# A Winograd-like 3x3 convolution with attention: its VectorE operations chained with the softmax, and a 1x1 convolution moved into the middle of the 3x3

## The chip, the cores and the metric

One core of a Trainium2 chip runs the kernel. The metric is device time in microseconds (us) from one launch; lower is better. The five engines each execute their own queue of instructions in the order in which they stand: TensorE (PE, with its weight loads shown apart as PEld), VectorE (DVE), ScalarE (ACT), GpSimd (POOL) and SyncE (SP, which here issues nearly all DMAs).

## The reference

Input x is 8 images of 512 channels, 32x32, in float32. Two layers run one after the other, each with a residual:

```python
x = x + L0(_gn(x))       # _gn: group normalization, 32 groups of 16 channels
x = x + L1(_gn(x))       # L1: one 1x1 convolution, weights scaled and masked by softmax gates, channels permuted

def L0(x):
    t = cbs(x, cv1_w, cv1_bn, 0)             # 1x1, batch norm, silu: 512 -> 512
    ys = [t[:, :256], t[:, 256:]]
    for i in range(2):                       # two blocks
        yi = ys[-1]
        z = cbs(yi, m_cv1_w[i], m_cv1_bn[i], 1)                    # 3x3, 256 -> 256
        z = bot_attention(z, m_qkv_w[i], m_rw[i], m_rh[i])         # 4 heads of 64, 1024 positions
        z = silu(bn_eval(conv2d(z, m_cv2_w[i], 0), m_cv2_bn[i]))   # 1x1, 256 -> 256
        ys.append(yi + z)
    return cbs(concatenate(ys), cv2_w, cv2_bn, 0)                  # 1x1, 1024 -> 512
```

The attention adds a position term to k, takes logits over 1024x1024 positions, a softmax over the keys and the product with v.

## The kernel before

Work is cut into 16 slots, one for each (image, block). Images go in pairs: (0, block 0), (1, block 0), (0, block 1), (1, block 1), then images 2 and 3, and so on. I number slots from 0, so that a slot s with s mod 4 of 2 or 3 is a block 1 slot. A slot's foreground is its attention, as four `Unit`s (two pairs of heads, two halves of the 1024 queries). For each of eight key tiles a unit does:

- `logits` (L487-505): two matmuls `lg` into two PSUM banks, two ScalarE copies to the SBUF tile `st` (L500), two VectorE maxima `mx` that read the same banks (L505).
- After tile 7, `top` and `spread`: TensorE transposes `mt` of `mx`, a VectorE reduction (L514), TensorE transposes `mb` (L521).
- `soften` (L523-531): VectorE adds the negated maximum to `st` (L525), ScalarE takes the exponential (L526), GpSimd accumulates the denominators `sum` (L531).
- `values` (L537): two matmuls into `po`. At the end come `den`, a ScalarE copy `rb` (L551), and VectorE's reciprocal and product (L556, L558).

Between these steps a filler, `slot_filler(s)` (L871-904), hands out TensorE work of other kinds, by a budget of estimated microseconds (`SHARE`, 103 in a slot): the next slot's 3x3 convolution (`conv3`) and q, k, v projections (`project`), the 1x1 convolution `conv_m2` behind a finished attention, and background items from `bg` (`conv1`, 1x1 `cv` from x; `conv2`, `cv` from y; `last`, `l`). Every `yield` hands the turn back with the estimated time of what was emitted.

`conv_m2(i)` has four tiles: two matmuls into a bank `m2` each (traced as four instructions, "m<-q"), a silu on ScalarE (`m2s`, L130), a VectorE residual add (L406) and a store. In the slots before a block 1 slot the filler runs conv_m2(0), which makes that slot's input image; conv_m2(1) belongs to the previous slot's image when that one was in block 1 (s mod 4 of 3 or 0). After it, `finishing` adds that image's `conv2` and `last` to the background list.

The 3x3 convolution is done as six products over transformed rows:

- `transform` (L236-268) makes eight VectorE operations on the padded image `ybuf`, as a `Spread`: due times by the emission clock, with `upto(n)` forcing the first n. L256-L257 make `a` and `b`, L258-L259 planes 1 and 2, L261-L262 `a2` and `b2`, L263-L264 planes 3 and 4. For a block 0 image two slots ahead it is scheduled at the end of the filler, 8 us later and 1.3 us apart, after `load_y` has issued the load of `ybuf`.
- `conv3` (L270-350) runs products 1, 2, 3, 4, 0, 5 in this order, each 12 matmuls into one bank ("m<-plane", twice as many instructions in the trace) with four yields in all. After product 2, L316 and L317 combine it with product 1 on VectorE, L319 and L320 start planes u0 and u5 on GpSimd, and L321 and L322 finish them on VectorE. L328-L329 combine products 3 and 4, a second `Spread` (L330-339) of four VectorE operations prepares the sums, L343 and L347 add products 0 and 5, and two silus on ScalarE finish `z` (L349).

What sets the order on an engine: the program is emitted in the order of these generators, and a scheduler then orders each engine's instructions by priority and readiness as it estimates it. Instructions can be tied by an explicit dependency without a semaphore. Before the change, only `mx` (L505) and `st` (L525) are tied so: each is kept behind the one that was emitted before it, by `in_turn` (L469-475).

Buffers: `ps_f` has five PSUM banks, which `lg`, `mt`, products, `m2`, `cv`, `l`, `qk`, `v` and `den` take in the order of emission; `po` and `mb` have their own. A new tile waits until the last reader of the bank's previous tile is done. Weights have four SBUF buffers. The core has one `ybuf`, four planes and three temporaries `wt`.

Of the kernel before, what the change touches and what calls it, by code (L numbers as in the profile page):

```python
# [17 lines left out]
ALU = mybir.AluOpType  # L18
AX = mybir.AxisListType
PSUM = bass.MemoryType.PSUM  # L20
IN_ORDER = mybir.DependencyInfo(mybir.DependencyClass.NoSync, mybir.DependencyReason.DATA)
# [18 lines left out]
def conv_preact_kernel(ctx: ExitStack, tc: tile.TileContext, x, cv1, cv2, mcv1, qkv, mcv2, bn, rw, rh, conv, s_in, t_in, out):  # L40
    nc = tc.nc
    stt = nc.vector.scalar_tensor_tensor
# [22 lines left out]
    def pair(p, tag, name):  # L65
        return p.tile([P, 2, HALF], F32, tag=tag, name=name)

    def bank(name):
        return ps_f.tile([P, HALF], F32, tag="bank", name=name)
# [10 lines left out]
    def weights(name, shape, src):  # L80
        t = wp.tile([P, *shape], F32, tag="w", name=name)
        load(t, src)
        return t
# [45 lines left out]
    def bn_silu(dst, src, col):  # L129
        nc.scalar.activation(dst, src, AF.Silu, bias=bn_b[:, col : col + 1], scale=bn_s[:, col : col + 1])  # L130
# [40 lines left out]
    def accumulate(ps, terms):  # L171
# [5 lines left out]
                yield 1.72  # L177
        return Whole(1.72)

    class Spread:  # L180


# [5 lines left out]
        def upto(self, n):  # L188
            while self.done < n:
                self.done += 1  # L190
                self.ops[self.done - 1]()

    class Image:
        def __init__(self, n):
# [75 lines left out]
        def conv3(self, i):  # L270
            n = self.n
            name = f"{n}_{i}"
            self.inputs.upto(3)
            t, d = self.t, self.d

            def plane():
                plane_count[0] += 1
                return planes[plane_count[0] % 4]

            def inner(u):  # L280
                return u[:, :, 1 : F + 1]

            def product(r, u):
                w = weights(f"w_m1_{name}_{r}", (IT, IT, 3, P), w_m1[i][r])
                ps = bank(f"m1_{name}_{r}")
                terms = [(c, dx) for c in range(IT) for dx in range(3)]
                for co in range(IT):
                    for j, (c, dx) in enumerate(terms):
                        nc.tensor.matmul(  # L289
                            ps[:, ts(co, 256)].rearrange("p (t x) -> p t x", x=F),  # L290
                            w[:, co, c, dx],
                            u[:, 9 * c : 9 * c + 8, dx : dx + F],
                            start=(j == 0),
                            stop=(j == len(terms) - 1),
                        )
                        if j % 3 == 2 and (co, j) != (1, 5):
                            yield 1.33
                self.ps = ps

            z = self.z = qp.tile([P, IT, HW], F32, tag="z", bufs=1, name=f"z_{name}")  # L300
            y4 = z.rearrange("p c (t j x) -> p (c t) j x", j=4, x=F)
            y = [y4[:, :, j] for j in range(4)]

            def tx(ap):
                return ap.rearrange("p (g x) -> p g x", x=F)

            mm, ss, dd = (pair(wm, q, f"{q}_{name}") for q in ("mm", "ss", "dd"))
            yield from product(1, t[1])
            nc.scalar.copy(mm[:, 0], self.ps)
            yield 1.33  # L310
            self.inputs.upto(4)
            yield from product(2, t[2])
            self.inputs.upto(8)
            a, b = t["a2"], t["b2"]

            nc.vector.tensor_tensor(ss[:, 0], mm[:, 0], self.ps, ALU.add)  # L316
            nc.vector.tensor_tensor(dd[:, 0], mm[:, 0], self.ps, ALU.subtract)  # L317
            u0, u5 = plane(), plane()
            nc.gpsimd.tensor_tensor(inner(u0), d[0], d[2], ALU.subtract)  # L319
            nc.gpsimd.tensor_tensor(inner(u5), d[5], d[3], ALU.subtract)  # L320
            stt(inner(u0), inner(u0), 4.0, a, ALU.mult, ALU.add)  # L321
            stt(inner(u5), b, -4.0, inner(u5), ALU.mult, ALU.add)  # L322
            yield 1.33
            yield from product(3, t[3])
            nc.scalar.copy(mm[:, 1], self.ps)
            yield 1.33
            yield from product(4, t[4])
            nc.vector.tensor_tensor(ss[:, 1], mm[:, 1], self.ps, ALU.add)  # L328
            nc.vector.tensor_tensor(dd[:, 1], mm[:, 1], self.ps, ALU.subtract)  # L329
            sums = Spread(  # L330
                [
                    lambda: stt(y[2], tx(ss[:, 1]), 4.0, tx(ss[:, 0]), ALU.mult, ALU.add),
                    lambda: nc.vector.tensor_tensor(ss[:, 0], ss[:, 0], ss[:, 1], ALU.add),
                    lambda: stt(y[1], tx(dd[:, 1]), 2.0, tx(dd[:, 0]), ALU.mult, ALU.add),
                    lambda: stt(dd[:, 0], dd[:, 1], 8.0, dd[:, 0], ALU.mult, ALU.add),
                ],
                1.0,
                1.3,
            )
            yield 1.33  # L340
            yield from product(0, u0)
            sums.upto(2)
            nc.vector.tensor_tensor(y[0], tx(self.ps), tx(ss[:, 0]), ALU.add)  # L343
            yield 1.33
            yield from product(5, u5)
            sums.upto(4)
            nc.vector.tensor_tensor(y[3], tx(self.ps), tx(dd[:, 0]), ALU.add)  # L347
            for co in range(IT):
                bn_silu(z[:, co], z[:, co], BN_M1 + IT * i + co)  # L349
            yield 1.33  # L350
# [103 lines left out]
        def last(self, h, xn):  # L454
            n = self.n
            for cp in range(2):
# [8 lines left out]
                        yield us  # L465
                load(out[n, cp, :, :, ts(h, HALF)], res)
                yield us

    turn = []  # L469

    def in_turn(instruction):

        if turn:
            tc.add_manual_dep(instruction.ins, turn.pop().ins.name, IN_ORDER, reason="order of the softmax")
        turn.append(instruction)


    class Unit:
# [8 lines left out]
        def logits(self, t):  # L487

            if t == 0:
                self.begin()  # L490
            lg = [bank(f"lg_{self.name}_{t}_{h}") for h in range(2)]
            for h in range(2):
                r = slice(HD * h, HD * h + HD)
                nc.tensor.matmul(  # L494
                    lg[h], self.k[r, ts(t, P)], self.q[r, self.hp, ts(self.half, HALF)], start=True, stop=True
                )
            st = pair(stp, "st", f"st_{self.name}_{t}")
            self.st.append(st)
            for h in range(2):
                nc.scalar.copy(st[:, h], lg[h])  # L500
            if t == 1:
                self.mx = pair(one, "mx", f"mx_{self.name}")
            for h in range(2 if t else 0):
                so_far = self.st[0] if t == 1 else self.mx
                in_turn(nc.vector.tensor_tensor(self.mx[:, h], so_far[:, h], lg[h], ALU.max))  # L505
# [353 lines left out]
    def call(f, *a):  # L859
        f(*a)  # L860
        return
        yield

    def finishing(im):


        bg.add(Second(im, 0), Second(im, 1), held.pop(), Last(im, 0))
        held.append(Last(im, 1))
        bg.prepare()

    def slot_filler(s):  # L871

        prev = slots[s - 1] if s else (None, 0)
        nxt = slots[s + 1] if s + 1 < len(slots) else (None, 0)
        todo, needed = [], 0.0

        def add(us, g):
            nonlocal needed
            todo.append((us, g))
            needed += us  # L880

        im, i = nxt
        add(8.0, bg.take(8.0))
        if im and i == 1:
            add(7.0, im.conv_m2(0))
            add(0.0, call(im.transform, 1, 3.0, 1.0))
            add(9.0, bg.take(9.0))
        if im:
            add(32.0, im.conv3(i))
        if prev[1] == 1:  # L890
            add(7.0, prev[0].conv_m2(1))
            add(0.0, call(lambda: finishing(prev[0])))
        elif im:
            add(7.0, bg.take(7.0))
        if im:
            add(21.0, im.project(i))
        if s + 2 < len(slots) and slots[s + 2][1] == 0:
            add(0.0, call(slots[s + 2][0].load_y))
            add(0.0, call(slots[s + 2][0].transform, 0, 8.0, 1.3))
        rest = SHARE - needed if im else 70.0  # L900
        if rest > 0:
            todo.append((rest, bg.take(rest, wait=True)))
        total = sum(c for c, _ in todo)
        return needed, total, todo
# [73 lines left out]
    before = None  # L978
    for s in range(len(slots)):
        needed, total, todo = slot_filler(s)  # L980
        state = {"done": 0.0}

# [55 lines left out]
    im = images[NB - 1]  # L1038
# [55 lines left out]
```

## Time and profile before

| | |
|---|---|
| time, median of 3 runs | 3335.23 us (3323.23 to 3340.18) |
| the profiled execution | 3329.67 us, span 3328.0 us |
| mean granted TensorE clock | 0.985 |
| slots 4, 5, 6, 7 (they begin at 983.1, 1166.1, 1358.8, 1552.3 us; slot 8 at 1737.7) | 183, 193, 194, 185 us |
| one L525 `st`, L505 `mx`, L526 exp, L500 copy | 1212, 680, 1056, 595 ns |
| one `sum` of POOL (L531) | 1327 ns |
| TensorE instruction 128x512, full clock, half clock | 429 ns, 853 ns |
| DVE transform ops L256, 257, 258, 259, 261, 262, 263, 264 | 973, 1049, 1117, 714, 1387, 1046, 1256, 918 ns |

In rows of the profile, "out<-in" are the program's tile names; the numbers behind a bar are busy time in us, mean ns of one, and idle time just before the group with the instructions that ended it. In the timeline a line gives start, length, engine, line, tiles and count; in square brackets stands the idle time before it and what released it. L175 is the line of a helper (`accumulate`) and L130 that of `bn_silu`, so these are told apart by tile names.

### The profile page before, as it was taken

Reading aid. Unit: us, or ns where it says so; the run is one execution under the profiler, and the core shown is the slowest. Engines: PE = TensorE matmul, PEld = TensorE weight load, DVE = VectorE, ACT = ScalarE, POOL = GpSimd, SP = SyncE. Lnnn points to the kernel's source line nnn. Section 1 sums busy time; section 2 is a strip of 40 time slices with the busy share of each in tenths; the row PEclk is TensorE's granted clock in tenths of the full one; section 3 lists DMA queues with packets and bytes.
Section 4 is the critical chain, followed back from the end, with each engine's and each line's share of the span. In section 5 each row is a group of like instructions: output and inputs, shape, how many; then the busy total and the mean of one; then the engine's idle time right before and its main releaser. Section 6 shows DMA issues by size and latency. Waiting matters only on the chain.

```text
span 3328.0 us, 33287 instructions
## 1 busy us (share of the span) xinstructions
PE 3177.4 (95%) x11716; PEld 1541.6 (46%) x11716; DVE 2069.0 (62%) x2717; ACT 1763.7 (53%) x2371; POOL 1238.7 (37%) x971
## 2 busy tenths in 40 slices
PE   7999989999999999999999999999999999999998
PEld 3645344354445444354445445354545445353343
DVE  5536566666656566666656665776756665766642
ACT  3245765854555654644455554644455554645631
POOL 2114333445334443444334333434334343444420
PEclk9999999999999999999999999999999999999999
DMA  8752442421132241423232341423232341423366
GB/s 293 263 170 70 144 147 86 136 83 54 67 129 83 93 138 49 158 82 121 82 124 86 112 145 54 153 88 111 92 117 92 117 141 52 158 70 108 111 212 207
DMA packets 142006, 399.29 MB, mean 120 GB/s; under 512 B 13072, under 2 KB 14352, under 8 KB 141840
## 3 DMA queue, kind: packets, MB, share of 16 engines
q1 hardware_dynamic: 141120, 396.94, 34.8%
q8 instruction: 93, 1.52, 0.2%
q14 instruction: 73, 0.60, 0.1%
q10 hardware_dynamic: 720, 0.23, 0.0%
HBM read 317.42 MB, written 79.69 MB: 119 GB/s over the span
## 4 chain that ended last, share of the span: by engine, by line
PE 69%; DVE 10%; issue 6%; ACT 5%; DMA 3%; POOL 1%; SPq 0%; POOLq 0%; DVEq 0%; ACTq 0%
PE cv L175 14%; PE po L537 11%; PE m L289 11%; PE lg L494 11%; PE qk L175 6%; PE l L175 6%; PE v L381 3%; DVE st L525 2%; PE mt L513 2%; PE den L549 2%; PE m L175 2%; DVE mx L505 2%; PE mb L521 2%; ACT st L526 1%; DVE rb L556 1%
## 5 line engine op out<-in xcount | busy, mean ns | idle before, releaser
L531 POOL TENSOR_TENSOR sum<-sum,st 128x512 f32<-128x512 f32 x768 | 995.7, 1327 | 762.6 <-ACT st L526 762.6
L526 ACT ACTIVATE st<-st 128x1024 f32<-128x1024 f32 x512 | 536.2, 1056 | 516.9 <-DVE st L525 509.6
L505 DVE TENSOR_TENSOR mx<-mx,lg 128x512 f32<-128x512 f32 x768 | 479.2, 680 | 412.6 <-ACT st L500 412.2
L525 DVE TENSOR_TENSOR st<-st,mb 128x1024 f32<-128x1024 f32 x512 | 604.4, 1212 | 88.3 <-PE mb L521 88.3
L500 ACT COPY st<-lg 128x512 f32<-128x512 f32 x1024 | 527.3, 595 | 205.5 <-PE lg L494 163.8
L289 PE MATMUL m<-plane,w_m 128*128 128x256 f32 x2304 | 540.3, 388 | 24.3 <-DVE mx L505 18.6
L494 PE MATMUL lg<-q,k 64*128 64x512 f32 x2048 | 538.4, 620 | 10.6 <-ACT y L130 3.4
L537 PE MATMUL po<-st,v 128*64 128x512 f32 x2048 | 511.5, 611 | 7.5 <-ACT st L526 5.1
L289 PEld LDWEIGHTS m<-plane,w_m 128*128 128x128 f32 x2304 | 434.7, 193 | 148.9 <-issue 52.7
L531 POOL TENSOR_TENSOR sum<-st,st 128x512 f32<-128x512 f32 x128 | 160.3, 1274 | 878.9 <-ACT st L526 617.1
L175 PE MATMUL cv<-y,w_cv 128*128 128x512 f32 x1024 | 467.3, 600 | 3.0 <-ACT m2s L130 1.3
L494 PEld LDWEIGHTS lg<-q,k 64*128 64x128 f32 x2048 | 189.8, 186 | 349.3 <-issue 218.2
L175 PEld LDWEIGHTS cv<-y,w_cv 128*128 128x128 f32 x1024 | 185.1, 190 | 251.0 <-issue 235.5
L537 PEld LDWEIGHTS po<-st,v 128*64 128x64 f32 x2048 | 125.7, 137 | 328.3 <-issue 250.0
L556 DVE RECIPROCAL rb<-rb 128x256 f32<-128x256 f32 x128 | 216.0, 1725 | 71.9 <-ACT rb L551 71.9
L175 PE MATMUL l<-x,w_l 128*128 128x512 f32 x512 | 239.5, 614 | 17.0 <-DVE mx L505 12.3
L175 PE MATMUL cv<-x,w_cv 128*128 128x512 f32 x512 | 237.1, 610 | 17.3 <-DVE mx L505 9.0
L175 PE MATMUL qk<-z,w_qkv 128*128 128x512 f32 x512 | 236.7, 604 | 10.5 <-DVE mx L505 10.5
L514 DVE TENSOR_REDUCE nm<-mt 128x4 f32<-128x512 f32 x128 | 83.2, 685 | 189.2 <-PE mt L513 189.2
L130 ACT ACT_TABLE_LOAD x123 | 157.8, 1283 | 19.0 <-PE cv L175 8.1
L175 PEld LDWEIGHTS l<-x,w_l 128*128 128x128 f32 x512 | 95.0, 194 | 141.2 <-issue 105.5
L175 PEld LDWEIGHTS cv<-x,w_cv 128*128 128x128 f32 x512 | 94.6, 193 | 140.8 <-issue 107.2
(144 smaller groups left out, 2372.6 us busy)
## 6 DMA issues: line engine op xcount, KB each, us to landing
w_m<-w_m SPq DMA_DIRECT2D x96, 768.0 KB, 4.3
w_cv<-in_cv SPq DMA_DIRECT2D x90, 512.0 KB, 3.5
y<-y SPq DMA_DIRECT2D x64, 512.0 KB, 4.9
x<-in_x SPq DMA_DIRECT2D x56, 512.0 KB, 5.1
y<-y SPq DMA_DIRECT2D x64, 256.0 KB, 3.8
k<-r SPq DMA_DIRECT2D x32, 512.0 KB, 3.6
res<-y SPq DMA_DIRECT2D x32, 512.0 KB, 4.1
xr<-in_x SPq DMA_DIRECT2D x32, 512.0 KB, 4.1
```

Source lines behind the costliest of these rows:

```text
L130: nc.scalar.activation(dst, src, AF.Silu, bias=bn_b[:, col : col + 1], scale=bn_s[:, col : col + 1])
L175: nc.tensor.matmul(ps, w, moving, start=(n == 0), stop=(n == len(terms) - 1))
L289: nc.tensor.matmul(ps[:, ts(co, 256)].rearrange("p (t x) -> p t x", x=F), w[:, co, c, dx], u[:, 9 * c : 9 * c + 8, dx : dx + F], start=(j ...
L381: nc.tensor.matmul(ps[:, ts(j, P)], z[:, c, ts(4 * j4 + j, P)], w[:, c, 512 + P * hp : 512 + P * hp + P], start=(c == 0), stop=(c == IT - 1),)
L494: nc.tensor.matmul(lg[h], self.k[r, ts(t, P)], self.q[r, self.hp, ts(self.half, HALF)], start=True, stop=True)
L500: nc.scalar.copy(st[:, h], lg[h])
L505: in_turn(nc.vector.tensor_tensor(self.mx[:, h], so_far[:, h], lg[h], ALU.max))
L525: in_turn(nc.vector.tensor_tensor(st, st, flat(self.mb), ALU.add))
L526: nc.scalar.activation(st, st, AF.Exp)
L531: nc.gpsimd.tensor_tensor(self.acc[:, h], so_far[:, h], self.st[t][:, h], ALU.add)
L537: nc.tensor.matmul(self.po[HD * h : HD * h + HD], self.v[:, t, ts(h, HD)], self.st[t][:, h], start=(t == 0), stop=(t == KT - 1),)
L556: nc.vector.reciprocal(self.rb[:, r], self.rb[:, r])
```

## The change

Two things are done. First, `in_turn` moves up, and the operations of every `Spread` (the eight transform operations and the four sums) as well as L321 and L322 pass through it: on VectorE these now keep the order of emission among themselves and with `mx` and `st`. L316, L317, L328, L329, L343, L347, L406 and the background's VectorE operations remain free.

Second, in the six slots that have both a previous block 1 image and a next slot (3, 4, 7, 8, 11, 12), the filler runs the first 16 yields of `conv3`, which are products 1, 2, 3 and 4, then conv_m2(1) with `finishing`, then products 0 and 5. Before, conv_m2(1) followed all six. In these slots a `bg.take(7.0)` is now put behind the products, and the rest that the slot's background takes shrinks by the same amount, since `needed` grows by 7.

```diff
+    turn = []
+
+    def in_turn(instruction):
+
+        if turn:
+            tc.add_manual_dep(instruction.ins, turn.pop().ins.name, IN_ORDER, reason="order of VectorE")
+        turn.append(instruction)
+
     class Spread:
...
             while self.done < n:
                 self.done += 1
-                self.ops[self.done - 1]()
+                in_turn(self.ops[self.done - 1]())
...
-            stt(inner(u0), inner(u0), 4.0, a, ALU.mult, ALU.add)
-            stt(inner(u5), b, -4.0, inner(u5), ALU.mult, ALU.add)
+            in_turn(stt(inner(u0), inner(u0), 4.0, a, ALU.mult, ALU.add))
+            in_turn(stt(inner(u5), b, -4.0, inner(u5), ALU.mult, ALU.add))
...
-    turn = []
-
-    def in_turn(instruction):
-
-        if turn:
-            tc.add_manual_dep(instruction.ins, turn.pop().ins.name, IN_ORDER, reason="order of the softmax")
-        turn.append(instruction)
-
...
-        if im:
-            add(32.0, im.conv3(i))
+        products = im.conv3(i) if im else iter(())
         if prev[1] == 1:
+            if im:
+                add(21.3, (us for _, us in zip(range(16), products)))
             add(7.0, prev[0].conv_m2(1))
             add(0.0, call(lambda: finishing(prev[0])))
-        elif im:
+        if im:
+            add(10.7 if prev[1] == 1 else 32.0, products)
             add(7.0, bg.take(7.0))
```

## The prediction

> **What bounds the kernel now.** I read the page's busy shares first, then its costliest groups, then the list of waits, and last the timeline around TensorE's longest gaps.
>
> ```profile
> span 3328.0 us, 33287 instructions
> PE 3177.4 (95%) x11716; PEld 1541.6 (46%) x11716; DVE 2069.0 (62%) x2717; ACT 1763.7 (53%) x2371; POOL 1238.7 (37%) x971
> PE 69%; DVE 10%; issue 6%; ACT 5%; DMA 3%; POOL 1%; SPq 0%; POOLq 0%; DVEq 0%; ACTq 0%
> L289 PE MATMUL m<-plane,w_m 128*128 128x256 f32 x2304 | 540.3, 388 | 24.3 <-DVE mx L505 18.6 <-DMA w_m<-w_m 3.4 <-issue 1.7
> L175 PE MATMUL m<-q,w_m 128*128 128x512 f32 x256 | 128.6, 649 | 18.2 <-ACT m2s L130 17.1 <-DVE mx L505 1.1
> ```
>
> TensorE is busy 95%; the change adds and removes no matmul, so it can work on the 150.6 us (3328.0 - 3177.4) in which PE is idle, and on matmul time run at a low clock. The last two rows say where idle time sits: the 3x3 products (L289) lose most before `mx` (L505, VectorE), the 1x1 `conv_m2` (L175, m<-q) before its own silu on ScalarE. The list of waits names who holds them:
>
> ```profile
> PE m L175 <- ACT m2s L130: 17.1, 6, 3.7
> DVE a L256 <- DMA ybuf<-y: 27.2, 8, 8.5
> DVE plane L321 <- POOL plane L319: 31.7, 12, 4.4
> ```
>
> The second row is VectorE waiting for an image load at the head of its queue, where `mx` is stuck behind it. The timeline shows each kind once, first slot 7's conv_m2(1), then slot 6's product 3:
>
> ```profile
> 1612.83 1.98 PE L175 MATMUL m<-q,w_m 128*128 128x512 f32 x4 [0.36 <-DVE mx L505]
> ...
> 1619.23 2.37 ACT L130 ACTIVATE z<-z,bn_b,bn_s 128x1024 f32<-128x1024 f32 x2
> 1621.51 0.76 ACT L130 ACTIVATE m2s<-m,bn_b,bn_s 128x512 f32<-128x512 f32 x1
> ...
> 1622.32 5.84 PE L175 MATMUL m<-q,w_m 128*128 128x512 f32 x7 [3.71 <-ACT m2s L130]
> ```
>
> ```profile
> 1436.87 0.74 DVE L256 SCALAR_TENSOR_TENSOR a<-ybuf 128x544 f32<-128x544 f32 x1 [3.66 <-DMA ybuf<-y]
> 1437.53 1.78 DVE L257 SCALAR_TENSOR_TENSOR b<-ybuf 128x544 f32<-128x544 f32 x1
> 1439.23 2.46 DVE L505 TENSOR_TENSOR mx<-mx,lg 128x512 f32<-128x512 f32 x4
> ...
> 1439.96 6.39 PE L289 MATMUL m<-plane,w_m 128*128 128x256 f32 x21 [4.21 <-DVE mx L505]
> ```
>
> In the first, conv_m2's second tile wants a PSUM bank whose silu stands behind the table load and the two `z` silus that end the 3x3. In the second, L256 of the next image's transform waits 3.66 us for its load, all four `mx` wait behind it, and with them the bank that product 3 needs. After the first gap seven L175 matmuls take 5.84 us (0.83 each), where four took 1.98 (0.5) before it: the clock had halved.
>
> **The Trainium skill.** "TensorE: Matmul & The Clock Gate", What's actually happening: the array falls to half clock after an idle window of about 3.4 us and returns after a busy one. The trace agrees on the halving (matmul spacing 429 ns against 853 ns, in stretches of 3.41 or 6.83 us) but gaps of 2.0 us (1056.4, 1811.0) were followed by one too, so I charge it for gaps of 2 us and more. "SBUF — State Buffer", SBUF: two separate sides: VectorE with two SBUF inputs and GpSimd exclude each other. The trace agrees: L257 takes 0.7 us alone and 1.79 us beside POOL's `sum`. "PSUM — Partial Sum Buffer", Terms: two engines on one bank at once are an error. So copies and `mx` of a bank must take turns; the trace has `mx` waiting 423.1 us, 173 times, for ACT's copies. A bank is thus free only when `mx` has read it: late VectorE work stalls TensorE.
>
> **The change part by part.** I compared the order of instructions on each engine in the two built programs with the gaps of the trace. SP's and POOL's orders stay nearly the same: only w_m2 and the two `res` loads come earlier, w_qkv later and the finished stores earlier, all loads of 3.5 to 5 us with a product (5.2 us) or more of lead. I cost them nothing; without that lead, one load is 4 us. "After" below stands for that order.
>
> A, conv_m2(1) between products 4 and 5 in slots 3, 4, 7, 8, 11, 12. (Product 0 runs after it too.) Removed: the waits on m2s, and later ones on `mx` held by L406's wait for m2s. The PE timeline gives 3.72, 3.72, 3.72 (867.4, 1622.3, 2376.8), 1.98 three times (1056.4, 1811.0, 2562.9) and 2.38, 3.50, 1.84 (1072.6, 1828.3, 2576.8): 24.8 us. Half-clock beside them: busy time inside the low stretches, halved, is 2.9 + 1.7 + 2.6 + 1.7 + 1.7 = 10.6. Added: after, the first tile follows the `mb` transposes while ACT is idle; the second takes the bank that lg_0_0 had, free after ACT's rb (0.58), table load (1.28), two exps (1.06 each) and a copy (0.60). Set against the PE work between, it comes about 1.3 us late: 6 x 1.3 = 7.8. Bounds: 0 (ACT starts earlier) to 3.7 (the old wait again), 0 to 22. Gain 24.8 + 10.6 - 7.8 = 27.6.
>
> B, the transform of the next image after the products instead of among them (slots 2, 6, 10): chained, L256 cannot stand ahead of these `mx`. Gone: 2.66 + 4.21 + 4.21 (708.5, 1440.0, 2194.5) = 11.1, and three half-clock stretches of 3.4 us, halved: 5.1. Gain 16.2. It is late next in E.
>
> C, slots 1, 5, 9: `mt` waits 4.6 us for `mx` behind L261, L262, L263 (1217.5, 1972.4, 2719.4). After, L263 (1.67 us there) stands behind the last `mx`: 3 x 1.67 = 5.0, and one or two of the three half-clock halves of 1.7: take 2.6. Gain 7.6 (0 to 10).
>
> D, slots 2, 6, 10: l waits 3.5 us behind L261, L258, L259 and L262 (1396.3, 2151.1, 2898.1). After, only L256 to L258 stand ahead, but the other five and the residual's L433 and L139 then precede the next two `mx`, and product 1 waits about 3.7 us for one of their banks. Its start was 1406.7 and becomes 1403.8 plus that wait's half clock of 1.7: net gain 1.2 each, 3.6 (-5 to 8).
>
> E, where the moved transforms land: the last of the four units. In slots 2, 6, 10 that unit's VectorE is idle only some 7.3 us of 1526 to 1550, and eight ops of 8.46 us (means of L256 to L264) come in. I find the second and third `l1` tiles waiting 2.2 and 2.5 us for banks, plus 0.8 of low clock: 5.5 x 3 = 16.5. In slots 3, 7, 11 with longer 1x1 tiles, 0.8 x 3 = 2.4. Loss 18.9; bounds: 0 (the room suffices) and twice that.
>
> F, the chain itself. L321 and L322 now stand in emission order, L322 ahead of `st` 6 and 7. In slot 7 POOL's L320 ended at 1578.43 and `st` 6 began at 1576.36; it would begin at 1580.1, and `mx` 6 and 7 move from 1583.1 to 1584.2. The bank is wanted at 1585.8: hidden, with about 1 us to spare. For spots like it that I missed I charge one VectorE op of 0.68 us for each of 15 convolutions: 10 us (0 to 20).
>
> Sum: 27.6 + 16.2 + 7.6 + 3.6 - 18.9 - 10 = 26 us less. The profiled execution took 3329.67 us, 1.7 outside its span; 3329.7 - 26 = 3304. The median shown is 3335.23, 5.6 above that execution: **3309**.
>
> **The rivals.**
> 1. Given back: A and B are gained, but E costs double (37.8) and A's new bank wait is like the old (3.3 each, 20). For: VectorE is at 62% over the whole, but nearly full in the last units. Against: some slack remains there. Sum of gains: 35.4 (A before its own new wait) + 16.2 - 20 + 11.2 (C, D) - 37.8 - 10 = -5, so 5 us slower, which is no change: 3340.
> 2. Slower, one mechanism: L322 at the head of VectorE's queue waits for POOL's L320, and `st` 6 and 7 wait behind it, then exp, `mx`, and the bank for product 4. The wait list above has L321 waiting 31.7 us for POOL already, 12 times, up to 4.4. If L320 sits behind one more pair of `sum` (2 x 1.33 = 2.7 us), 1.0 is hidden and 1.7 shows, with 1.7 of half clock: 3.4 for each of 15, 51. Behind two pairs 4.3 + 1.7, 90. Between them 70 against the 36 before F: 3335 + 34 = 3369. It decides from about 36 / 15 = 2.4 us per convolution, L320 some 2 us later than now. Against: POOL's order stays, and it is idle 63%.
> 3. The conv_m2 move does nothing since ACT's queue holds m2s in its new place too, while B to F hold: -26 + 27.6 = +2, 3337. It is counted with the first.
>
> **How the numbers follow.** Forecast 0.52; given back, with the third, 0.25; slower 0.23. The unknown costs, each at its bad end, give 12 + 11 + 0 - 5 - 38 - 20 = 40 us slower; at the good end 35 + 16 + 10 + 8 = 69 faster. They won't all fall together: I take 60 faster to 23 slower than 3335, 3275 to 3358, leaving out most of the slower case. Half a per cent, 16.7 us, is about what can be told from no change here. Faster by more: most of the forecast and a little of the second: 0.54; within: 0.23; slower: 0.23.
>
> **What would show it.** A: in L175's m<-q row the 17.1 us on m2s falls under 8, and no 3.7 us gap stands in slots 3, 7, 11. B: L256's wait for ybuf (27.2) no longer has PE gaps after it. C: `mt`'s 13.8 us falls to 9 or less. E: new `l` gaps behind `mx` late in slots 2, 6, 10. F: L322 behind L320 waits longer, but PE gaps before product 4 stay absent. I am wrong if PE idle grows beyond 150.6, above all with `st` L525 late in products 2 to 4 of every slot.

## The result and the profile after

The changed kernel takes 3281.7 us (median of 5 runs, 3278.47 to 3286.18) against 3335.23; the ratio is 0.9845 (95% interval 0.9826 to 0.9865). Its profiled execution has a span of 3276.7 us, 51.3 less. I number lines as in the kernel after where its rows are shown: before's L256-L264 are L264-L272, L289 is L297, L316-L317 are L324-L325, L321-L322 are L329-L330, L332-L335 are L340-L343, L343 is L351 and L406 is L414.

The page's first lines, and the rows of the list of groups that answer to those of before:

```profile
span 3276.7 us, 33257 instructions
PE 3159.1 (96%) x11716; PEld 1538.0 (47%) x11716; DVE 2045.9 (62%) x2717; ACT 1756.6 (54%) x2369; POOL 1219.1 (37%) x971
```

```profile
L297 PE MATMUL m<-plane,w_m 128*128 128x256 f32 x2304 | 534.0, 386 | 18.0 <-DVE z L351 8.3 <-DVE mx L505 6.2 <-DMA w_m<-w_m 2.8
L175 PE MATMUL m<-q,w_m 128*128 128x512 f32 x256 | 121.4, 614 | 4.0 <-ACT st L500 4.0
L513 PE MATMUL mt<-ident,mx 128*128 128x128 f32 x512 | 73.3, 288 | 10.7 <-DVE mx L505 10.7
```

The same matmuls are executed. TensorE's idle time fell from 150.6 to 117.6 us (3276.7 - 3159.1), 33.0; its busy time fell by 18.3, and the granted clock tells why: halving the busy time inside each half-clock stretch gives 47.4 us lost before and 30.1 after. The 3x3 now loses 6.2 us on `mx` instead of 18.6, and conv_m2 nothing on its silu instead of 17.1. New are 8.3 us in which the 3x3 waits for L351, VectorE's addition of product 0. In the list of waits the load at the head of VectorE's queue is rare now, and GpSimd hardly holds VectorE:

```profile
DVE a L264 <- DMA ybuf<-y: 8.4, 1, 8.4
DVE plane L329 <- POOL plane L327: 3.6, 1, 3.6
DVE plane L330 <- POOL plane L328: 0.6, 1, 0.6
```

The timeline of slot 7's conv_m2(1), where the gap of 3.71 us had been:

```profile
1576.18 1.88 PE L175 MATMUL m<-q,w_m 128*128 128x512 f32 x4
...
1578.10 0.78 ACT L130 ACTIVATE m2s<-m,bn_b,bn_s 128x512 f32<-128x512 f32 x1 [8.78 <-PE m L175]
...
1579.14 0.58 ACT L551 COPY rb<-den 128x512 f32<-128x512 f32 x1 [0.27 <-PE den L549]
1579.75 1.28 ACT L526 ACT_TABLE_LOAD   x1
...
1580.92 1.99 PE L175 MATMUL m<-q,w_m 128*128 128x512 f32 x4
1581.04 2.00 ACT L526 ACTIVATE st<-st 128x1024 f32<-128x1024 f32 x2
1582.95 2.02 ACT L500 COPY st<-lg 128x512 f32<-128x512 f32 x4
...
1583.57 3.70 PE L175 MATMUL m<-q,w_m 128*128 128x512 f32 x8 [0.67 <-ACT st L500]
```

ScalarE sat idle for 8.78 us before the first `m2s`, so it runs at once. After it come rb, a table load, two exps and the copies, and the third of the four tiles waits for a copy: 0.67 us in place of 3.71, and too short for the clock to drop.

Summed by slot (the start of a slot is its first `mt`), the gain lies so:

```
slots                  predicted (A to E, without F)      measured
3, 4, 7, 8, 11, 12     A 27.6 - E 2.4            = 25.2       25.9
2, 6, 10, 14           B 16.2 + D 3.6 - E 16.5   =  3.3       15.7
5, 9, 13               C                            7.6       10.8
0, 1, 15, before 0     none                                   -1.1
```

A slot's length is not waiting alone, since TensorE work moves between slots too: busy time without the half-clock loss is 1.7 us less in the first row and 2.6 less in the third, and 4.0 more in the second.

### The profile page after: what moved, and what is told of

Read it like the earlier page. It is cut to its first block, busy times and chain, and to the rows that moved or that the text cites. A ratio compares the mean times of both kernels' runs of the same rounds, so it can differ in the third digit from the quotient of the medians.

```text
span 3276.7 us, 33257 instructions
## 1 busy us (share of the span) xinstructions
PE 3159.1 (96%) x11716; PEld 1538.0 (47%) x11716; DVE 2045.9 (62%) x2717; ACT 1756.6 (54%) x2369; POOL 1219.1 (37%) x971
## 3 DMA queue, kind: packets, MB, share of 16 engines
q1 hardware_dynamic: 141120, 396.94, 36.1%
## 4 chain that ended last, share of the span: by engine, by line
PE 69%; DVE 11%; issue 5%; ACT 4%; DMA 4%; POOL 1%; POOLq 0%; SPq 0%; ACTq 0%; DVEq 0%
PE cv L175 14%; PE m L297 12%; PE po L537 11%; PE lg L494 10%; PE qk L175 6%; PE l L175 5%; PE v L389 3%; DVE st L525 3%; PE mt L513 2%; PE m L175 2%; DVE rb L556 2%; DVE mx L505 2%; PE den L549 2%; PE mb L521 2%; DMA x<-in_x 1%
## 5 line engine op out<-in xcount | busy, mean ns | idle before, releaser
L531 POOL TENSOR_TENSOR sum<-sum,st 128x512 f32<-128x512 f32 x768 | 973.9, 1299 | 771.5 <-ACT st L526 771.5
L297 PE MATMUL m<-plane,w_m 128*128 128x256 f32 x2304 | 534.0, 386 | 18.0 <-DVE z L351 8.3
L297 PEld LDWEIGHTS m<-plane,w_m 128*128 128x128 f32 x2304 | 431.4, 191 | 142.7 <-issue 40.8
```

What stands on the lines that cost most here:

```text
L297: nc.tensor.matmul(ps[:, ts(co, 256)].rearrange("p (t x) -> p t x", x=F), w[:, co, c, dx], u[:, 9 * c : 9 * c + 8, dx : dx + F], start=(j ...
L531: nc.gpsimd.tensor_tensor(self.acc[:, h], so_far[:, h], self.st[t][:, h], ALU.add)
```

## The experiments

Each was timed against the kernel before on the same chip; ratios have 95% intervals. The kernel before has medians from 3333.01 to 3336.06 us on the chips used, so a difference of two or three us between versions from different chips says nothing.

**The two edits apart.** First the chain, with the filler as before:

```diff
-        products = im.conv3(i) if im else iter(())
+        if im:
+            add(32.0, im.conv3(i))
         if prev[1] == 1:
-            if im:
-                add(21.3, (us for _, us in zip(range(16), products)))
             add(7.0, prev[0].conv_m2(1))
             add(0.0, call(lambda: finishing(prev[0])))
-        if im:
-            add(10.7 if prev[1] == 1 else 32.0, products)
+        elif im:
             add(7.0, bg.take(7.0))
```

> The chained VectorE order alone; conv_m2(1) stays behind all six products, without the extra background take. Theory 1 (the two edits work in different slots and add): the gain of slots 5, 6, 9, 10, 13, 14 and 2 stays, about 26 us, and that of slots 3, 4, 7, 8, 11, 12, also about 26, goes: near 3309 us, ratio 0.992, with TensorE gaps of about 3.7 us before conv_m2's second tile in slots 3, 7, 11. Theory 2 (the order carries all, the move is idle without need): near 3283, 0.985. Theory 3 (the move carries all): near 3335, 1.00.

Measured: 3298.57 us, ratio 0.9897 (0.9883 to 0.9912). Then the filler's edit alone, with only `mx` and `st` chained.

> The move of conv_m2(1) with the extra background take alone; only mx and st are chained, as before. Theory 1 (the edits add): near 3309, 0.992, with mt still waiting about 4.6 us in slots 5, 9, 13 and l about 3.5 us in slots 6, 10, 14. Theory 2 (the order carries all): near 3335. Theory 3 (the move carries all): near 3283.

Measured: 3305.04 us, 0.9916 (0.9901 to 0.9931). So neither edit carries all. By slots, slots 2, 5, 6, 9, 10, 13 and 14 gain 28.1 us with the chain alone and lose 3.1 with the move alone; slots 3, 4, 7, 8, 11, 12 gain 29.3 with the move alone and 8.9 with the chain alone. The gains overlap: 35.8 + 29.3 = 65.1 against 52.7 with both (3334.37 - 3281.7). The timeline of the chain-only kernel, slot 7, shows where:

```profile
1604.58 2.37 ACT L130 ACTIVATE z<-z,bn_b,bn_s 128x1024 f32<-128x1024 f32 x2
1606.86 0.76 ACT L130 ACTIVATE m2s<-m,bn_b,bn_s 128x512 f32<-128x512 f32 x1
...
1607.67 4.56 PE L175 MATMUL m<-q,w_m 128*128 128x512 f32 x10 [2.31 <-ACT m2s L130]
```

The same wait on m2s behind the `z` silus, 2.31 us here and 3.71 before: the chain shortens by 1.4 a wait that the move takes away whole. My expectation of 3.7 there was wrong, and with it that the edits merely add.

**Is it the place or the extra take?** The chain, the extra 7 us of background in the six slots, and conv_m2(1) after all six products:

```diff
-        products = im.conv3(i) if im else iter(())
+        if im:
+            add(32.0, im.conv3(i))
         if prev[1] == 1:
-            if im:
-                add(21.3, (us for _, us in zip(range(16), products)))
             add(7.0, prev[0].conv_m2(1))
             add(0.0, call(lambda: finishing(prev[0])))
         if im:
-            add(10.7 if prev[1] == 1 else 32.0, products)
             add(7.0, bg.take(7.0))
```

> The changed kernel, but conv_m2(1) stays behind all six products; the extra background take of 7 us stays between it and the projections. If the place of conv_m2 gives the gain in slots 3, 4, 7, 8, 11, 12: near 3309, with the 3.7 us gaps before its second tile back. If the extra take gives it, by putting other matmuls between the last product and what waits for z: near 3285, and qk's waits stay away.

Measured: 3304.97 us, 0.9917 (0.9900 to 0.9933): the take without the move gains nothing over the chain alone (3298.57). The complement keeps the move and leaves the take out:

```diff
             add(10.7 if prev[1] == 1 else 32.0, products)
-            add(7.0, bg.take(7.0))
+            if prev[1] != 1:
+                add(7.0, bg.take(7.0))
```

> The changed kernel without the 7 us of background that the change puts between product 5 and the projections in slots 3, 4, 7, 8, 11, 12. If that take is idle for the time: 3282, within 6. If it covers the wait for z's silus (qk after product 5): 3292 or more, with qk waits back. If it costs, as 3304.97 against 3298.57 of the two runs with conv_m2 at the end hints: near 3276.

Measured: 3268.35 us, 0.9806 (0.979 to 0.9822), 13.4 below the changed kernel's median. The take is a loss inside the change. Part of it is seen in slot 8. The changed kernel's timeline there:

```profile
1783.12 3.16 DVE L414 TENSOR_TENSOR res<-res,m2s 128x512 f32<-128x512 f32 x2 [1.56 <-DMA res<-y]
...
1786.20 1.21 DVE L525 TENSOR_TENSOR st<-st,mb 128x1024 f32<-128x1024 f32 x1
1787.34 0.68 DVE L351 TENSOR_TENSOR z<-m,ss 128x512 f32<-128x512 f32 x1
...
1788.07 4.15 PE L297 MATMUL m<-plane,w_m 128*128 128x256 f32 x18 [2.12 <-DVE z L351]
```

conv_m2's residual add waits for its load, `st` waits behind it, L351 behind that, and product 5 needs the bank that L351 reads. Without the take the adds take 1.29 us together, beside no GpSimd sum, and L351 comes in time:

```profile
1777.88 1.29 DVE L414 TENSOR_TENSOR res<-res,m2s 128x512 f32<-128x512 f32 x2 [1.59 <-DMA res<-y]
...
1781.35 0.69 DVE L351 TENSOR_TENSOR z<-m,ss 128x512 f32<-128x512 f32 x1
...
1782.09 4.15 PE L297 MATMUL m<-plane,w_m 128*128 128x256 f32 x18 [0.29 <-DVE z L351]
```

In both, the load of `res` comes late by the same amount (1.56 and 1.59 us); what differs is how long the adds behind it take.

The profiled executions differ by only 6.8 us (3276.7 and 3269.9), but slots 3, 4, 7, 8, 11 and 12, where the take was, are 10.9 us shorter together. The stretch before slot 0, which the edit leaves as it was, is 5.0 longer; half clock costs 5.1 more there.

**Is it ScalarE's queue?** conv_m2(1) between products 0 and 5:

```diff
-                add(21.3, (us for _, us in zip(range(16), products)))
+                add(26.7, (us for _, us in zip(range(20), products)))
...
-            add(10.7 if prev[1] == 1 else 32.0, products)
+            add(5.3 if prev[1] == 1 else 32.0, products)
```

> The changed kernel with conv_m2(1) between products 0 and 5 in place of 4 and 0. If the old wait came only from z's two silus and the table load standing before m2s on ScalarE: as good, 3282 within 6, conv_m2's gaps about 0.7. Rival: the place matters by what stands around it in the unit (the mb transposes, rb, the sums on VectorE): 3292 or more, with other gaps in slots 3, 4, 7, 8, 11, 12 only.

Measured: 3291.84 us, 0.9874 (0.9858 to 0.9891). In between: 13 us of the 23 that the place is worth stay (3304.97 to 3281.7). The silus of `z` come after conv_m2 here too, and its gap is 1.4 us (`mx`), with another of 1.3 before `mt` in slots 4, 8 and 12. The old wait on m2s is gone with the silus, as A argued; the other 10 belong to what else stands around the new place, of which these gaps are what the trace shows.

**What of the chain does it?** The eight transform operations chained, the four sums and L329, L330 (u0, u5) free:

```diff
-                in_turn(self.ops[self.done - 1]())
+                self.tie(self.ops[self.done - 1]())
...
-            in_turn(stt(inner(u0), inner(u0), 4.0, a, ALU.mult, ALU.add))
-            in_turn(stt(inner(u5), b, -4.0, inner(u5), ALU.mult, ALU.add))
+            stt(inner(u0), inner(u0), 4.0, a, ALU.mult, ALU.add)
+            stt(inner(u5), b, -4.0, inner(u5), ALU.mult, ALU.add)
```

Here `tie` is `in_turn` for the transform and does nothing for the sums.

> The changed kernel with the eight transform operations alone chained; the four sums and L321, L322 free. If the order of the transform carries the chain's gain, as B, C and D said: 3282 within 6. If the chained sums carry a part: the wait of about 2.0 us before a product in slots 5, 9, 13 (1262.4 in the profile of before) is back, 3 x (2.0 + 0.7) = 8: near 3291.

Measured: 3292.99 us, 0.9882 (0.9865 to 0.9899): 11.3 of the chain's gain need the other operations. And with only u0 and u5 free:

> The changed kernel, but L321 and L322 (planes u0 and u5, waiting for GpSimd) not chained. If their place costs nothing, as step F said: 3282, within 8 us, and no new gaps around product 3 and 4. If the rival's mechanism is there in part, hidden under larger gains, freeing them gains: 3272 or less. If the chain of these two is itself part of the gain: 3292 or more.

Measured: 3286.03 us, 0.9859 (0.9843 to 0.9874), the interval overlapping the changed kernel's. With the move in place the steps are then 3305.04 with nothing but `mx` and `st` chained, 3292.99 with the transform too, 3286.03 with the sums too, 3281.7 with u0 and u5 too. The last step, 4.3 us, is not clear of the noise by these times, but the traces show something of it.

In the transform-only kernel B's gaps of 4.21 us in slots 6 and 10 are gone, and `mt` (3.58 us) and `l` (1.12 to 1.40) wait about as in the changed kernel. Two kinds of waits are there that the changed kernel lacks: 2.05 us before a product in slots 5, 9 and 13 (2.04 in slot 2 too), and 1.07 us before `lg` in slots 6, 10 and 14. With u0 and u5 alone free, the first are gone and the second (1.06) are there. So the order of the sums removes the first, and that of u0 and u5 the second. In the list of waits u0's operation with u0 and u5 free has

```profile
DVE plane L329 <- POOL plane L327: 36.1, 15, 5.1
```

where the changed kernel has 3.6. How the sums do it shows in slot 9 of the transform-only kernel (its rows from L347 on are numbered one higher):

```profile
1978.55 1.21 DVE L526 TENSOR_TENSOR st<-st,mb 128x1024 f32<-128x1024 f32 x1
...
1981.00 3.37 POOL L532 TENSOR_TENSOR sum<-sum,st 128x512 f32<-128x512 f32 x2 [4.22 <-ACT st L527]
1981.48 1.77 DVE L342 SCALAR_TENSOR_TENSOR z<-dd 128x512 f32<-128x512 f32 x1
...
1983.17 1.75 DVE L341 TENSOR_TENSOR ss<-ss 128x512 f32<-128x512 f32 x1
...
1985.44 1.21 DVE L526 TENSOR_TENSOR st<-st,mb 128x1024 f32<-128x1024 f32 x1
...
1988.99 3.25 PE L297 MATMUL m<-plane,w_m 128*128 128x256 f32 x8 [2.05 <-DVE mx L506]
```

and the changed kernel in the same place:

```profile
1977.70 0.69 DVE L343 SCALAR_TENSOR_TENSOR dd<-dd 128x512 f32<-128x512 f32 x1
1978.31 2.35 DVE L525 TENSOR_TENSOR st<-st,mb 128x1024 f32<-128x1024 f32 x2
1979.37 1.99 PE L494 MATMUL lg<-q,k 64*128 64x512 f32 x8
...
1981.29 5.86 PE L297 MATMUL m<-plane,w_m 128*128 128x256 f32 x24
```

Free, the first of two `st` goes ahead of the sums, and the second stands behind all four. GpSimd's `sum`, which follows the first `st`, then runs beside two of the sums, which take 1.77 and 1.75 us; the second `st` begins at 1985.44, when the logits are done. Its exp (1986.68) stands ahead of ScalarE's copies of these logits (1987.65), and `mx` waits for the copies. Chained, the sums come first and take 0.68 or 0.69 each, and the two `st` follow, the first of them 1.06 us before the logits begin. The bank waited for 2.05 us is free in time.

**Two versions that go on.** C had named L261 and L262 (after: L269, L270) ahead of the last `mx`. I drew the block 1 transform apart:

```diff
-            add(0.0, call(im.transform, 1, 3.0, 1.0))
+            add(0.0, call(im.transform, 1, 3.0, 2.5))
```

> The changed kernel with the block 1 transform's eight operations 2.5 us apart in place of 1.0. If mt's 3.57 us waits in slots 5, 9, 13 come from L261 and L262 of that transform standing before the last mx: they fall to 1.5 or less, each with its half clock, 3 x (2 + 2) = 12 us: near 3270. Rival: what is taken from there is waited for by the products that need planes 3 and 4: new gaps before product 3, 3282 or more.

Measured: 3273.04 us, 0.9823 (0.9803 to 0.9843), 8.7 below the changed kernel's median. The 3.57 us waits of `mt` are gone from slots 5, 9 and 13, which are 3.6, 2.7 and 3.7 us shorter; product 1 waits 1.7 there instead. With the extra take left out as well:

> The changed kernel with both edits that had made it faster: no extra take in slots 3, 4, 7, 8, 11, 12, and the block 1 transform's operations 2.5 us apart. They touch different slots: if they add, 3281.7 - 13.4 - 8.7 = 3260, within 6; if they meet in the same waits, no better than the better one, 3268.

Measured: 3256.02 us (3250.31 to 3256.87), 0.9755 (0.9732 to 0.9778). The two add, and this version beats both kernels.

```diff
-            add(0.0, call(slots[s + 2][0].transform, 0, 8.0, 1.3))
+            add(0.0, call(slots[s + 2][0].transform, 0, 8.0, 2.6))
```

> The same, and the block 0 transform's operations 2.6 us apart in place of 1.3. If the waits of 0.85 and 1.46 us of l and po late in slots 6 and 10 (step E of the prediction) come from these operations standing close together before mx: they go, 2 x 2.3 = 5 us, and in slots 3, 7, 11 nothing changes: 4 to 5 below the run beside it. If the unit has no room for them anyway, or conv3's start takes them all at once: no change, or slower by the waits of product 1.

Measured: 3255.8 us, 0.9759 (0.9736 to 0.9783), the same. In slots 6 and 10 the waits of 0.86 and 1.46 became one of 1.39, and these slots were 2.0 and 2.8 us shorter; slots 3, 4 and 15 were 1.8, 1.3 and 4.2 us longer. The order there was not worth the effort.

## Why the prediction was right, and where its sum was not

The direction and most places were right, the size half: 26 us forecast, 51.3 in the profiled executions, 53.5 between the medians. Point by point, idle time and half clock from the two profiles:

- **A** held: 24.7 of 27.6. The named gaps (24.8) and their half-clock (10.6) are gone. For the new wait I had put 7.8; there are 4.0 (six of 0.67, before the third tile and not the second), but also two of 2.12 before product 5 and three of 0.82 before `po`, together 10.7. So A's total came out near with other waits than the one it charged for, which is in part luck. The two of 2.12 touch "I cost them nothing": the `res` load arrives 1.56 us late at the head of VectorE's queue. But the load is as late without the take, and in slot 8 only 0.29 us is left there, so the load alone doesn't make the wait. Alone, the move gained 29.3 us in these slots.
- **B** held: the gaps of 2.66, 4.21 and 4.21 us are gone, and 4.85 of half clock (5.1 forecast).
- **C** was too large: `mt` waits 3.57 us in place of 4.6, 3.1 us for three slots, not 5.0, and the half-clock stretches did not go: 7.3 us lost beside these waits against 5.0. Its sign, `mt` at 9 us or less, was missed: 10.7. What failed is the size of its term: L263's place was put at 1.67 us a slot and gave 1.0, without the half clock. L261 and L262 (after: L269, L270) still stand before the last `mx`; with the transform spread the wait goes. (C named slots 1, 5, 9 and D slots 2, 6, 10; the times that they quote lie in slots 5, 9, 13 and 6, 10, 14.)
- **D** was too small. `l` waits 1.34, 0.58 and 1.35 us in place of 3.5, and product 1 waits 1.35 where I had put 3.7. The idle time saved is 3.2; and all three half-clock stretches, 8.8 us of loss, went with it: 12.0 against 3.6. D had a charge for a new stretch and no term for those that would go.
- **E** was mis-sized: 18.9 forecast. In slots 6 and 10, `po` waits 0.85 and `l` 1.46, 2.3 where I had 5.5; in slot 2, it is 5.0 more, at waits of `po` that I had not named; in slots 3, 7, 11 0.7 each. With 1.2 more of half clock in slot 2 this makes 12.9. The chain's loss beside the move in slots 3, 4, 7, 8, 11 and 12 was 3.4 (29.3 - 25.9). VectorE had more room than E thought: in slot 6's last unit (1526 to 1550 before, 1507 to 1531 after) its busy time rises from 17.20 to 21.39 us of 24, with six of the eight operations, 6.7 us, in that window. (Before, 6.8 us were idle, not 7.3.)
- **F**, the 10 us charged for the chain itself, had the wrong sign: with u0 and u5 free the kernel was not faster, and the waits of 1.07 us in slots 6, 10 and 14 came back, 3.2 us. The order of the sums, which no step of the prediction prices, removed the waits of 2.05 us in slots 5, 9 and 13, 6.1 us. That is 9.3 us gained where 10 were charged; the transform-only chain, 11.3 us slower, agrees.

Against the sum of 26, then: the charge F, +10; the sums, u0 and u5, +9; D, +8; E, +6; C, A and B together, -10. That is 49, against 51.3; smaller waits that came or went, such as 0.66 us before product 5 in slots 6, 10 and 14, are not in it.

The slower rival did not come about. Its sign would have been VectorE waiting at L322 for GpSimd, and that wait came to 0.6 us in all; L321's shrank from 31.7 to 3.6, and is 36.1 with the two free. Kept to their place in emission, they come up after GpSimd is done; F and the rival had them come up before. In rival 1, the new bank wait was less than that forecast (0.67 against 1.3), not more.

## What to carry to other kernels

When one engine is busy 95% and its waits are on buffers that another engine frees, look at what stands ahead of the freeing instruction in that engine's queue; an order written out for those instructions can be worth a per cent without one operation saved (here 35.8 of 3334.37 us for the chain alone). Here a scheduler's order by its own estimate put operations that were not urgent, one of them waiting for a load, ahead of the reads that free banks. And test the parts of a change by themselves even when the whole is a gain: here one part, an extra stretch of background work, was costing 11 to 13 us.

## What had not been expected of the hardware

A gap of TensorE much shorter than the 3.41 us that a half-clock stretch lasts can bring one on, and the gap's length alone does not decide. Over the twelve profiles from slot 0 on (before, after and ten experiments), counting a gap as followed by low clock when a half-clock stretch begins between 1 us before it and 3.6 us after its end:

```
gap, us        gaps   followed by half clock
0.6 to 1.0      294      0
1.0 to 1.5      103      7
1.5 to 2.0       96     23
2.0 to 2.5       62     27
2.5 to 3.0       31     26
3.0 to 4.0       50     45
over 4.0         26     26
```

The prediction charged every gap of 2 us and more; up to 2.5 us fewer than half of them paid. What decides is the phase. In each profile all half-clock stretches begin on one grid of 3.413 us, to within 5 ns. Take the windows of that grid in the same twelve profiles, from slot 0 on, at full clock, and TensorE's idle time inside each:

```
idle in the window, us     windows   followed by half clock
under 1.0                    10160      0
1.0 to 2.0                     277     38
2.0 and more                   117    116
```

So a gap of 2.5 us can go unpaid when the edge of a window divides it, and one of 2.1 us be paid for when it lies within a window. In the kernels before and after, a stretch of 3.41 us costs some 1.7 us (half of it) and one of 6.83 us 2.6 to 3.4. A wait cut from 3.5 to 1.4 us, as in D, can save more by the clock (8.8 us over three slots) than by its length (3.2 with the new waits taken off).
